# Two unused tiles ahead of the operands of a convolution's matrix products

## The chip, the core and the metric

The kernel runs on one core of a Trainium2 chip. The metric is the time of the whole program on the device in microseconds, from one launch, as the median of several runs. Before the change it is 2550.75 us (three runs, 2549.53 to 2551.24). A profile of one more execution comes with it. "PE" is the TensorE matrix engine, "PEld" the loading of its weights, "DVE", "ACT", "POOL" and "SP" are the vector, scalar, GpSimd and sync engines.

SBUF, the on-chip memory, has 128 partitions. A tile takes the same range of bytes in every partition, and "the start" of a tile is here always its byte in the partition.

## The reference

Three conv layers (and one small "interval" layer between the second and the third) act on x of 4 images, 32 x 32 pixels, 16 channels, each behind a group norm, each added back to x:

```python
first = jnp.einsum('ijyx,byxc->bijc', Msq, inputs)
kern = jnp.transpose(G, (0, 1, 5, 4, 2, 3)).reshape(h * w * f, c, G.shape[2], G.shape[3])
shifted = lax.conv_general_dilated(x_nchw, kern, STRIDES, PADDING)      # h*w*f = 16384 filters of 3x3x16
diff = jax.nn.relu(inputs[:, None, None, :, :, :] - shifted)
second = L * jnp.einsum('ijyx,bijyxc->bijc', Wsq, diff)
return first - second
```

So every one of the 1024 pixels (i, j) has 16 filters of its own (3 x 3 x 16 taps); each filter is run over the whole image, the difference to the image goes through a relu, and is summed over all pixels with a weight. The filters' products are nearly all the arithmetic.

## The kernel before

**Phases and steps.** There are 6 phases: 3 layers by 2 groups of two images. A phase has 8 chunks of 128 output pixels (t), a chunk 32 steps (f, b): one of 16 filters by one of the two images of the group. That is 6 x 8 x 32 = 1536 steps. A step computes the products of 128 filters (one for each pixel of the chunk, as the columns of the weights) with 1024 image positions, into a pair of PSUM banks `ps` (128 x 2 x 512).

**The products** (`products`, L591 to L606). The contraction over 9 x 16 = 144 taps and channels is held in 128 partitions, as two halves of 64 rows; half `h` of the rows makes one half of the image. Each product is one matmul with 64 rows, 128 weight columns and 512 moving columns (480 for one half of the last product), in the fp32r format. The two halves use different rows of the array and are issued one after the other. Numbers are split into a coarse and a fine part to keep precision, so a step has seven pairs of matmuls: `first_part` (L608) issues four pairs, weights WU and WL against the moving tiles `iy` and `iz`; then ACT scales the PSUM result (L628); one step later `second_part` (L631) issues three more, weights WD against `iyz` and W9 against `im9`, and DVE reduces the result with the relu and the weights `WT` in one instruction (L644). The order on PE is thus four pairs of step n, three pairs of step n-1, and so on, without a break. The first 16 steps use another form, with plain fp32 products from the tiles `first` and `raw` (L616).

**The moving operands** are the tiles `iy`, `iz`, `iyz` (for each of two groups 2 slots x 2 images x 512 floats, 8192 bytes) and `im9` (2 images x 512 floats, 4096 bytes), all from the pool `const`. They are computed once a phase from the tile `raw` (L120).

**The weights** of four filters are a unit. A unit has a tile `parts` (L217: 2 slots x 3 kinds x 4 filters x 128 floats, 12,288 bytes) and a tile `W9` (L218: 4 filters x 128 floats), three buffers of each, in the pool `wpool`, which also holds the loaded filters (`raw_u`, L107, two buffers) and the chunks `WT` (L113). A filter's weights of one kind are 512 bytes. `prep_parts` (L211) makes them from the loaded filters with ACT, DVE and POOL and two DMAs (L238), ahead of their use, and issues the next load (L108).

**Where tiles stand.** The pools take SBUF in the order in which they are opened, and within `const` tiles follow each other in the order of their lines. The program's own constants and a descriptor area come first, up to byte 16,512; then X (two tiles of 1024 bytes), XQ (1024) and raw (13,056). So `iy0` starts at 32,640. From there on, tile after tile of `const` up to L740 and later, then the pools `wpool`, `work`, `ivp` and `big`. `WT`, `W9`, `raw_u` and `parts` start at 101,824 and at whole multiples of 2048 from it. The last byte used is 223,296.

The lines that the change stands among:

```python
L120    raw = const.tile([P, 3, GB, PITCH], F32, name="raw")
L121    iy = [const.tile([P, 2, GB, NH], F32R, name=f"iy{g}") for g in range(NG)]
L124    im9 = [const.tile([P, GB, NH], F32R, name=f"im9{g}") for g in range(NG)]
L217            parts = wpool.tile([P, 2, 3, FU, P], F32R, tag="parts", bufs=AHEAD + 1, name=f"parts_{u}")
```

Of the kernel before, what the change touches and what calls it, by code (L numbers as in the profile page):

```python
# [8 lines left out]
F32 = mybir.dt.float32  # L9
# [6 lines left out]
P = 128  # L16
# [26 lines left out]
def net_kernel(ctx: ExitStack, tc: tile.TileContext, x, xq, xi, convs, iv_w, iv_b, out):  # L43
# [29 lines left out]
    const = ctx.enter_context(tc.tile_pool(name="const", bufs=1))  # L73
# [44 lines left out]


    raw = const.tile([P, 3, GB, PITCH], F32, name="raw")  # L120
    iy = [const.tile([P, 2, GB, NH], F32R, name=f"iy{g}") for g in range(NG)]  # L121
    iz = [const.tile([P, 2, GB, NH], F32R, name=f"iz{g}") for g in range(NG)]
    iyz = [const.tile([P, 2, GB, NH], F32R, name=f"iyz{g}") for g in range(NG)]
    im9 = [const.tile([P, GB, NH], F32R, name=f"im9{g}") for g in range(NG)]  # L124


    F0 = 2
# [819 lines left out]
```

## Time and profile before

| what | us |
|---|---|
| median of three runs | 2550.75 |
| the profiled execution's own time | 2549.96 |
| its span, first to last instruction | 2548.2 |
| PE busy in it | 2533.8 |
| PEld busy | 2182.0 |
| DVE busy | 2079.2 |
| ACT busy | 1893.1 |
| POOL busy | 1103.8 |

The span is what the views of the trace divide up; 1.8 us lie around it. Busy times are unions of overlapping instructions: the pipelined matmuls overlap each other, so the mean duration of a matmul (about 390 ns) is not the time from one to the next. For that one reads start times.

### The profile page before, as it was taken

To read this page: it belongs to the slowest core of one execution; us is meant where nothing else is said; L and a number is where in the kernel's file an instruction comes from. 1 tells how busy PE (TensorE), PEld (TensorE's weight loads), DVE (VectorE), ACT (ScalarE), POOL (GpSimd) and SP (SyncE) were. 2 spreads that over 40 slices of the span, in tenths; PEclk is the share of its full clock that TensorE was granted. 3 is DMA by queue.
4 is the path that set the end of the run, shared out by engine and by line. 5 is a ranking of instruction groups with operands and counts; after the bars stand their busy time and mean duration, and the time that the engine had idled before them with its cause. 6 is when DMAs were issued, how large, how long until landed. Compare 5 with 4: busy or idle time off the path is not lost.

```text
span 2548.2 us, 56662 instructions
## 1 busy us (share of the span) xinstructions
PE 2533.8 (99%) x21906; PEld 2182.0 (86%) x21906; DVE 2079.2 (82%) x3621; ACT 1893.1 (74%) x2181; POOL 1103.8 (43%) x990
## 2 busy tenths in 40 slices
PE   8999999999999999999999999999999999999999
PEld 5999888888888888998888888888888888888887
DVE  8887777888777887777788888888888887777777
ACT  4777777777777777777777777777777777777776
POOL 3445333453333434333345555454646344333332
PEclk9999999999999999999999999999999999999999
DMA  5556345464444654444454444554444466354442
GB/s 171 182 148 171 112 133 141 114 168 136 131 136 130 196 161 120 136 130 130 133 141 133 132 116 135 144 154 130 122 134 135 130 164 199 110 142 133 133 133 53
DMA packets 81182, 353.80 MB, mean 139 GB/s; under 512 B 18448, under 2 KB 20368, under 8 KB 80144
## 3 DMA queue, kind: packets, MB, share of 16 engines
q1 hardware_dynamic: 79920, 349.57, 49.0%
q8 instruction: 172, 2.82, 0.5%
q14 instruction: 98, 0.80, 0.1%
q10 hardware_dynamic: 864, 0.58, 0.1%
q0 software_dynamic: 128, 0.02, 0.0%
HBM read 199.19 MB, written 0.98 MB: 79 GB/s over the span
## 4 chain that ended last, share of the span: by engine, by line
PE 99%; ACT 0%; DVE 0%; issue 0%; POOL 0%; DVEq 0%; ACTq 0%; POOLq 0%
PE pc L599 98%; PE pf L396 1%; ACT pc L628 0%; PE ps_l L519 0%; PE ps_r L532 0%; DVE junk L644 0%; ACT L562 0%; ACT L324 0%; DVE raw L815 0%; PE ps_y L583 0%; DVE kept L759 0%; DVE kept L755 0%; PE ps_v L769 0%; DVE raw L823 0%; DVE squares L792 0%
## 5 line engine op out<-in xcount | busy, mean ns | idle before, releaser
L644 DVE SCALAR_TENSOR_TENSOR junk<-pc,WT 128x1024 f32<-128x1024 f32 x1536 | 1880.1, 1224 | 444.1 <-PE pc L599 404.3
L628 ACT ACTIVATE pc<-pc 128x1024 f32<-128x1024 f32 x1520 | 1531.8, 1008 | 621.9 <-PE pc L599 597.2
L599 PE MATMUL pc<-iyz,parts 64*128 64x512 f32 x6080 | 990.7, 393 | 1.8 <-ACT pc L628 1.8
L599 PE MATMUL pc<-iz,parts 64*128 64x512 f32 x6080 | 989.8, 392 | 0.0
L599 PE MATMUL pc<-iy,parts 64*128 64x512 f32 x6080 | 977.4, 390 | 0.0
L599 PEld LDWEIGHTS pc<-iyz,parts 64*128 64x128 f32 x6080 | 622.6, 185 | 96.7 <-ACT pc L628 5.6
L599 PEld LDWEIGHTS pc<-iz,parts 64*128 64x128 f32 x6080 | 619.9, 185 | 92.3
L599 PEld LDWEIGHTS pc<-iy,parts 64*128 64x128 f32 x6080 | 615.3, 185 | 90.2 <-issue 4.4
L228 POOL TENSOR_TENSOR parts<-raw,upper_w 128x512 fp32r<-128x512 f32 x190 | 246.7, 1298 | 1022.1 <-PE pc L599 863.0
L599 PE MATMUL pc<-im,W 64*128 64x512 f32 (+1 forms) x3072 | 631.9, 390 | 0.0
L599 PEld LDWEIGHTS pc<-im,W 64*128 64x128 f32 x3072 | 315.3, 185 | 49.8 <-issue 3.2
L229 POOL TENSOR_TENSOR W<-W,raw 128x512 fp32r<-128x512 f32 x190 | 247.9, 1305 | 2.0 <-ACT W L170 1.9
L232 POOL TENSOR_TENSOR parts<-parts 128x512 fp32r<-128x512 f32 x190 | 246.6, 1298 | 2.8 <-ACT parts L227 2.5
L205 POOL TENSOR_TENSOR raw<-raw,ident 128x512 f32<-128x512 f32 x190 | 201.1, 1059 | 43.1 <-DMA raw<-in_g 35.2
L170 ACT ACTIVATE W<-raw,low_w 128x512 fp32r<-128x512 f32 x190 | 136.1, 716 | 1.1 <-DMA raw<-in_g 1.1
L644 DVE DVE_READ_ACCUMULATOR junk<-pc,WT 128x1 f32 x1536 | 127.6, 83 | 0.0
L227 ACT ACTIVATE parts<-upper_w 128x512 fp32r<-128x512 f32 x190 | 118.7, 625 | 3.4 <-DVE upper_w L194 3.4
L231 ACT CAST parts<-upper_w 128x512 fp32r<-128x512 f32 x190 | 116.8, 615 | 0.0
L659 POOL TENSOR_SCALAR acc<-acc 128x32 f32<-128x32 f32 x40 | 11.5, 288 | 168.3 <-DVE junk L644 163.8
L194 DVE TENSOR_SCALAR upper_w<-raw 128x512 int32<-128x512 int32 x190 | 82.2, 433 | 0.2
L551 POOL TENSOR_TENSOR tables<-ft_b,rt 128x1089 f32<-128x1089 f32 x16 | 37.7, 2355 | 0.3 <-DVE s_b L558 0.3
L551 POOL TENSOR_TENSOR tables<-ft_a,rt 128x1089 f32<-128x1089 f32 x16 | 37.7, 2354 | 0.0
(138 smaller groups left out, 395.0 us busy)
## 6 DMA issues: line engine op xcount, KB each, us to landing
raw<-in_g SPq DMA_DIRECT2D x190, 768.0 KB, 7.2
parts<-parts SPq DMA_DIRECT2D x380, 384.0 KB, 5.0
WT<-in_w SPq DMA_DIRECT2D x48, 512.0 KB, 4.6
MT<-in_mt SPq DMA_DIRECT2D x6, 2048.0 KB, 13.5
raw<-xs SPq DMA_DIRECT2D x120, 67.8 KB, 2.6
raw<-in_xi SPq DMA_DIRECT2D x3, 271.0 KB, 5.0
raw<-in_xi SPq DMA_DIRECT2D x1, 813.0 KB, 6.9
xs<-xt SPq DMA_DIRECT2D x20, 34.0 KB, 2.3
```

Source lines behind the costliest of these rows:

```text
L170: nc.scalar.activation(dst, src, AF.Copy, scale=mask[:, 1:2])
L194: nc.vector.tensor_scalar(t.bitcast(I32), src.bitcast(I32), HIGH, None, op0=ALU.bitwise_and)
L205: eng.tensor_tensor(raws[u][:, s, at:to], raws[u][:, s, at:to], pick[s][:, f0 + at : f0 + to].unsqueeze(2).to_broadcast([P, to - at, P]), ...
L227: nc.scalar.activation(WD, high, AF.Copy, scale=-EPS)
L228: nc.gpsimd.tensor_tensor(WL, w8, high, ALU.subtract)
L229: nc.gpsimd.tensor_tensor(W9, W9.bitcast(F32), src[:, 2], ALU.add)
L231: nc.scalar.copy(WU, high)
L232: nc.gpsimd.tensor_tensor(WD, WD.bitcast(F32), WL.bitcast(F32), ALU.add)
L551: nc.gpsimd.tensor_tensor(t, ft[:, i, :].unsqueeze(1).to_broadcast([P, T1, T1]), rt, ALU.add,)
L599: nc.tensor.matmul(ps[:, half, :n], lhsT=w[r], rhs=v[r] if n == NH else v[r][:, :n], start=first and k == 0, stop=k == len(pairs) - 1, ski ...
L628: nc.scalar.activation(ps, ps, AF.Copy, scale=1.0 + EPS)
L644: nc.vector.scalar_tensor_tensor(junk, ps.rearrange("p h n -> p (h n)"), 0.0, chunks[n], op0=ALU.min, op1=ALU.mult, accum_out=accs[phase][ ...
```

## The change

A tile of 32 floats (128 bytes in each partition) is put behind `raw`, and one of 112 floats (448 bytes) behind `im9`. Nothing writes or reads them. No instruction is added, removed or moved in its engine's order; every tile behind a new one starts later by the bytes of it.

```diff
     raw = const.tile([P, 3, GB, PITCH], F32, name="raw")
+    const.tile([P, 32], F32, name="pad")
     iy = [const.tile([P, 2, GB, NH], F32R, name=f"iy{g}") for g in range(NG)]
     iz = [const.tile([P, 2, GB, NH], F32R, name=f"iz{g}") for g in range(NG)]
     iyz = [const.tile([P, 2, GB, NH], F32R, name=f"iyz{g}") for g in range(NG)]
     im9 = [const.tile([P, GB, NH], F32R, name=f"im9{g}") for g in range(NG)]
+    const.tile([P, 112], F32, name="pad_parts")
```

| tile | start before | over a multiple of 2048 / 512 | start after | over a multiple of 2048 / 512 |
|---|---|---|---|---|
| raw | 19,584 | 1152 / 128 | 19,584 | 1152 / 128 |
| iy0 (iy1, iz, iyz, im9 follow at multiples of 4096) | 32,640 | 1920 / 384 | 32,768 | 0 / 0 |
| WT (W9, raw_u, parts follow at multiples of 2048) | 101,824 | 1472 / 448 | 102,400 | 0 / 0 |
| acc, junk, upper | 165,344 and on | 1504 / 480 | 165,920 and on | 32 / 32 |
| first, MT (the pool `big`) | 190,528 | 64 / 64 | 191,104 | 640 / 128 |

The last byte used becomes 223,872.

## The prediction

> **What bounds the kernel now.** First the page: busy times (part 1) and the chain that ended last (part 4).
>
> ```profile
> PE 2533.8 (99%) x21906; PEld 2182.0 (86%) x21906; DVE 2079.2 (82%) x3621; ACT 1893.1 (74%) x2181; POOL 1103.8 (43%) x990
> ...
> PE 99%; ACT 0%; DVE 0%; issue 0%; POOL 0%; DVEq 0%; ACTq 0%; POOLq 0%
> ```
>
> PE is on the chain for 99% of the span: the time is the number of products times the distance from one to the next. Next the groups of PE by shape, for how many there are, and the longest waits of PEld, for who could hold PE up:
>
> ```profile
> L599 PE MATMUL pc<-iyz,parts 64*128 64x512 f32 x6080 | 990.7, 393 | 1.8 <-ACT pc L628 1.8
> L599 PE MATMUL pc<-iz,parts 64*128 64x512 f32 x6080 | 989.8, 392 | 0.0
> L599 PE MATMUL pc<-iy,parts 64*128 64x512 f32 x6080 | 977.4, 390 | 0.0
> ...
> L599 PE MATMUL pc<-im,W 64*128 64x512 f32 x1536 | 613.4, 399 | 0.0
> L599 PE MATMUL pc<-im,W 64*128 64x480 f32 x1536 | 585.2, 381 | 0.0
> ```
>
> ```profile
> PEld pc L599 <- issue: 18.6, 74, 0.7
> PEld pc L599 <- ACT pc L628: 5.6, 10, 0.8
> ...
> PEld pc L599 <- DMA parts<-parts: 0.4, 1, 0.4
> ```
>
> 3 x 6080 + 2 x 1536 = 21,312 products, so 10,656 pairs of row halves. Another engine or a DMA holds them up for some 10 us in all. The distance is read from a timeline of PE in a quiet stretch (start, duration, group; groups merged):
>
> ```profile
> 632.24 0.63 PE L599 MATMUL pc<-iy,parts 64*128 64x512 f32 x4
> 632.70 0.64 PE L599 MATMUL pc<-iz,parts 64*128 64x512 f32 x4
> 633.16 0.64 PE L599 MATMUL pc<-iyz,parts 64*128 64x512 f32 x4
> 633.63 0.40 PE L599 MATMUL pc<-im,W 64*128 64x512 f32 x2
> 633.86 0.63 PE L599 MATMUL pc<-iy,parts 64*128 64x512 f32 x4
> ...
> 635.48 0.63 PE L599 MATMUL pc<-iy,parts 64*128 64x512 f32 x4
> ```
>
> Steps begin at 632.24, 633.86 and 635.48: 1.62 us for seven pairs, 231.4 ns a pair. From the start times of all products I worked out the distance between the first `iy` products of a step and of the step after next: it is 3240 ns, to the nanosecond, in 1368 of 1530 cases. 10,656 x 231.4 = 2466 us of the span of 2548.2; the start, the interval layer's and the first terms' products and the tail are the rest.
>
> Last the windows, where other traffic varies (PE, PEld, DVE, ACT, POOL, clock, DMA share, GB/s):
>
> ```profile
> 300.00:400.00 100.00, 100.00 (x868) 84.76 (x866) 78.88 (x131) 75.56 (x87) 39.55 (x36) 1.00 0.46 129
> 500.00:600.00 100.00, 100.00 (x866) 84.47 (x864) 81.93 (x137) 77.92 (x91) 51.14 (x45) 1.00 0.56 151
> 800.00:900.00 100.00, 100.00 (x867) 84.72 (x865) 81.55 (x150) 74.56 (x86) 37.38 (x38) 1.00 0.60 180
> 1200.00:1300.00 100.00, 100.00 (x868) 89.99 (x866) 80.81 (x145) 75.35 (x86) 41.38 (x43) 1.00 0.47 133
> ```
>
> 866 to 868 products begin in each 100 us, with DMA at 0.46 or 0.60 and POOL at 37 or 51 us. The last row has another overlap of the weight loads of the two halves (90 us of PEld in place of 85), and the same rate.
>
> **What the Trainium skill says.** "SBUF — State Buffer", section "Who interferes with whom", says that PE never waits on another engine for SBUF; the windows agree. The same page, "Specifications (TRN2)", gives lines of 16 bytes as the unit of SBUF reads. The old starts, 1920 and 1472 over a multiple of 2048, are already multiples of 64, so by it nothing is gained; no run here tests coarser units. "TensorE: Matmul & The Clock Gate", section "LDWEIGHTS (loading the stationary operand)", gives columns / 1.2 ns for a weight load, 107 ns for 128; the trace has 185, start to end. Its section "Back-to-back issue gap" gives N / 2.4 + 2.5, 216 ns for 512 columns; the trace has 231.4. So 15 ns a pair, 164 us in all, are above what that page would have. If the change moves the time, it is out of these.
>
> **The change part by part.** *The tiles.* No instruction, DMA or wait is added, and none is moved in an engine's order: 0 us. The starts do become what is said: 32,640 + 128 is 16 x 2048, and 101,824 + 576 is 50 x 2048, with tiles that are themselves multiples of 2048. `WT`, `W9` and `raw_u` move along with `parts`.
>
> *DVE, ACT, POOL.* Their instructions on moved tiles (1224, 1008 and 1298 ns) might change by some ns. DVE has 18% of the span free, ACT 26%, POOL 57%, and PE hardly waits for them: 0 us. Without that cover, a DVE instruction 10 ns longer would cost 1536 x 10 ns = 15 us; it would have to grow by some 250 ns to use up its free time.
>
> *DMAs.* A load of `raw_u` lands in 7.2 us, and a unit lasts 8 x 1.62 = 13 us. A transfer could become shorter or longer by a good part and PE would see 0.4 us of it: 0 us.
>
> *The moving operands.* The trace before has only starts of 1920 over a multiple of 2048 here, so this must be bounded. Within this, tiles of group 0 and 1 lie 8192 bytes apart, slots 4096, images 2048. Sorted by these, the mean distances (of those under 260 ns) from one product of a half to its next agree within 0.01 ns for the two groups, and the sum of both halves' for the two images of the first product within 0.05. Higher address bits do nothing, then. For misaligned reads there are the plain products of the first 16 steps, whose rows of 32 floats lie 136 bytes apart. PEld there:
>
> ```profile
> 17.90 0.23 PEld L599 LDWEIGHTS pc<-raw,first 64*128 64x128 f32 x2
> 18.33 0.23 PEld L599 LDWEIGHTS pc<-raw,first 64*128 64x128 f32 x2 [0.20 <-issue]
> 18.76 0.23 PEld L599 LDWEIGHTS pc<-raw,first 64*128 64x128 f32 x2 [0.20 <-issue]
> ```
>
> A pair is 0.43 us, and each product has two records. "FP8 and Floating Point Precision", "TensorE Precision Notes", says that true FP32 takes four passes, so a record holds two and a pass of 512 columns takes 215 ns, though its rows start anywhere. That is less than the 231 here. I take 0; from below, removing all of the 15 ns would give -164 us; from above, +2.5 ns a pair (below).
>
> *The weights.* The four filters of a unit start at 1472, 1984, 448 and 960 over a multiple of 2048. One of them crosses a multiple of 2048 inside, the others don't. The mean distances for the four are 231.46, 231.46, 231.46 and 231.47 ns. What isn't seen is a start at a multiple of 512: all have 448 over it; the loads from `first` (64 over it) mostly take 186 ns in place of 185. All loads of 128 columns in this trace start 64 or 32 over a multiple of 128. A load starts 2 to 3 ns after the product before it on its half, and the next product 228 to 233 ns after that load's start, so a shorter load may well show in the distance. I take 0, and for the ends a load of 183 ns, the lower value that recurs in the trace (-2 ns a pair, -21 us), and +2.5 ns a pair (+27 us).
>
> The sum is 0. On the profiled execution this is 2549.96 us, 0.8 below the median; on the median, 2550.7.
>
> **How small is measurable.** About 0.2% (5.1 us) is what a measurement here can tell from no change. It is 0.48 ns a pair. So PE's rhythm is either untouched, or what it moves by will be seen.
>
> **Rivals.** *A: the weight load gets shorter.* A start at a multiple of 512 saves a part of the read, 185 to 183 ns. For: loads stand in the chain from product to product, and there are 15 ns above the page's gap. Against: `first` at another remainder has the same load time, and two different overlaps of loads give the same 3240 ns. Time: 2550.7 - 21 = 2529; up to 16 ns would be 2380, which needs the whole gap.
>
> *B, slower: the two reads of a half begin at the same place.* A load starts 2 to 3 ns after a product. Before, weights and moving operand stood 448 and 384 over a multiple of 512, 64 bytes apart; after, both at 0. If PE's two reads of the same partitions disturb each other at equal places, the start of each pair is late. Distances of 231 and 236 ns alternate already in the trace, so a step of 5 ns exists in this machinery. Price: half of the 231 become 236, 2.5 ns a pair, +27 us, 2577; all of them, about 2600. It decides from 0.48 ns a pair on. Against: the four places of a filter change the distance between the two reads by 512 bytes each with no effect[...].
>
> *C: transfers into the moved tiles take another time.* Hidden under a unit's 13 us: 2550.7, the same as the forecast.
>
> *D: the tiles don't stand where said.* Excluded by the sums above.
>
> **How the numbers follow.** No change 0.50 (C in it), A 0.20, B 0.30. I give B more than A because any disturbance of a rhythm that repeats to the nanosecond can lock it into a longer one, while A needs the load to be what is shortened. Within 0.2% is the first case. The range takes the first case, A down to a little below its price, and B up to its price of 2.5 ns: 2528 to 2578, which leaves out some 2 in 10 (a longer gain, or a step of more than 2.5 ns). The likeliest case alone would be 2549 to 2552.5.
>
> **What would show it.** Right: in the profile after, steps 1.62 us apart, 866 to 868 products per 100 us, loads of 185 ns. A: loads of 183 ns or fewer, steps of 1.606 us or less. B: loads of the same time, steps of 1.637 us or more, and more distances of 236 ns. If DVE, ACT or DMA stand in the chain of waits after, what I called hidden was not. I am wrong if the rhythm depends on address bits between 64 and 1024, which this trace cannot show.

## The result and the profile after

The changed kernel takes 2525.39 us (median of 4 runs, 2524.39 to 2525.67), against 2550.35 for the kernel before (4 runs); the ratio is 0.9902, with a 95% interval of 0.9889 to 0.9914. It is faster by 25 us, 1%. The forecast was no change; the time lies 2.6 us below the stated range.

The page of the changed kernel, busy times and the chain that ended last (lines are two further down in this kernel, so L599 is L601 here):

```profile
PE 2509.2 (99%) x21906; PEld 2186.7 (87%) x21906; DVE 2080.3 (82%) x3621; ACT 1890.2 (75%) x2181; POOL 1103.6 (44%) x990
...
PE 99%; ACT 0%; DVE 0%; issue 0%; POOL 0%; DVEq 0%; ACTq 0%; POOLq 0%
```

PE is still the whole chain, with the same number of instructions. Its busy time fell by 24.6 us, the span by 24.3; DVE, ACT and POOL are where they were. The longest waits of PEld in the changed kernel:

```profile
PEld pc L601 <- issue: 19.3, 73, 0.7
PEld pc L601 <- ACT pc L630: 5.8, 10, 0.8
```

PE's loads wait for other engines about as long as before. Next the timeline of PE, in a stretch that answers to that of before:

```profile
630.35 0.63 PE L601 MATMUL pc<-iy,parts 64*128 64x512 f32 x4
...
631.93 0.66 PE L601 MATMUL pc<-iy,parts 64*128 64x512 f32 x4
...
633.55 0.63 PE L601 MATMUL pc<-iy,parts 64*128 64x512 f32 x4
```

The steps now take 1.58 and 1.62 us in turn. There are 1520 steps of this form, so 1518 distances from a step to the step after next (the prediction's 1530 is 12 too many). They are 3206 or 3207 ns in 1378 cases, where it was 3240 in 1368. Of a step's two halves one has a product of 480 columns, and which half it is changes from step to step, so two steps are the unit in which the rhythm repeats. The mean of those 1378 is 3206.7 ns: 33.3 ns less for two steps, and 760 such pairs of steps make 25.3 us, the whole of the gain. The windows of the changed kernel, by the columns of before:

```profile
300.00:400.00 100.00, 100.00 (x876) 86.93 (x876) 79.65 (x133) 76.22 (x87) 39.58 (x36) 1.00 0.47 130
500.00:600.00 100.00, 100.00 (x874) 86.61 (x872) 82.83 (x139) 78.78 (x92) 51.26 (x46) 1.00 0.57 156
800.00:900.00 100.00, 100.00 (x877) 86.97 (x876) 82.80 (x157) 76.53 (x88) 40.55 (x37) 1.00 0.58 172
1200.00:1300.00 100.00, 100.00 (x877) 86.99 (x875) 83.03 (x156) 75.82 (x87) 39.81 (x41) 1.00 0.49 137
```

874 to 877 products begin in 100 us, where it was 866 to 868, with the granted clock at 1.00 in both and whatever the DMA share. So the gain is there throughout the run. It is not the same for all seven pairs of a step: in the start times, averaged over the undisturbed steps, the time from the second `iz` pair to the first `iyz` pair fell from 233.3 to 225.5 ns, and that from the first `iy` pair to the second rose from 229.7 to 233.7. The weight loads:

```profile
L601 PEld LDWEIGHTS pc<-iz,parts 64*128 64x128 f32 x6080 | 624.3, 184 | 85.7
L601 PEld LDWEIGHTS pc<-iy,parts 64*128 64x128 f32 x6080 | 619.6, 184 | 78.2 <-issue 4.4 <-DVE junk L646 2.1
```

These take 184 ns in place of 185. On these views rival A (shorter loads at multiples of 512) looks right, with its price of 21 us for 25. The experiments show that it isn't.

### The profile page after: what moved, and what is told of

Read it like the earlier page. It is cut to its first block, busy times and chain, and to the rows that moved or that the text cites. A ratio compares the mean times of both kernels' runs of the same rounds, so it can differ in the third digit from the quotient of the medians.

```text
span 2523.9 us, 56662 instructions
## 1 busy us (share of the span) xinstructions
PE 2509.2 (99%) x21906; PEld 2186.7 (87%) x21906; DVE 2080.3 (82%) x3621; ACT 1890.2 (75%) x2181; POOL 1103.6 (44%) x990
## 4 chain that ended last, share of the span: by engine, by line
PE 99%; ACT 0%; DVE 0%; issue 0%; POOL 0%; DVEq 0%; ACTq 0%; POOLq 0%
PE pc L601 97%; PE pf L398 1%; ACT pc L630 0%; DVE junk L646 0%; PE ps_l L521 0%; PE ps_r L534 0%; ACT L326 0%; ACT L564 0%; DVE raw L817 0%; PE ps_y L585 0%; DVE kept L761 0%; DVE kept L757 0%; PE ps_v L771 0%; DVE raw L825 0%; DVE squares L794 0%
## 5 line engine op out<-in xcount | busy, mean ns | idle before, releaser
L601 PE MATMUL pc<-iy,parts 64*128 64x512 f32 x6080 | 988.7, 393 | 0.1
L601 PE MATMUL pc<-iyz,parts 64*128 64x512 f32 x6080 | 971.8, 389 | 1.9 <-ACT pc L630 1.9
L601 PE MATMUL pc<-iz,parts 64*128 64x512 f32 x6080 | 968.3, 387 | 0.0
L601 PEld LDWEIGHTS pc<-iz,parts 64*128 64x128 f32 x6080 | 624.3, 184 | 85.7
L601 PEld LDWEIGHTS pc<-iyz,parts 64*128 64x128 f32 x6080 | 611.9, 184 | 89.1 <-ACT pc L630 5.8
L601 PEld LDWEIGHTS pc<-iy,parts 64*128 64x128 f32 x6080 | 619.6, 184 | 78.2 <-issue 4.4
L601 PE MATMUL pc<-im,W 64*128 64x480 f32 (+1 forms) x3072 | 623.4, 384 | 0.0
L601 PEld LDWEIGHTS pc<-im,W 64*128 64x128 f32 x3072 | 311.4, 185 | 46.3 <-issue 3.4
```

Of the source, the lines that this page charges most:

```text
L601: nc.tensor.matmul(ps[:, half, :n], lhsT=w[r], rhs=v[r] if n == NH else v[r][:, :n], start=first and k == 0, stop=k == len(pairs) - 1, ski ...
```

## The experiments

All edits are to the kernel before, and only move tiles; the arithmetic is untouched. "Distance" is the start of the weights minus the start of the moving operands. It was 64 bytes modulo 512, and became 0. "Two steps" is the mean of the distances from a step to the step after next that recur in the profile of the run, read from the start times of PE; two values are given where stretches of the same run differ, and a bracket where it takes four steps for the rhythm to repeat. Ratios are against the kernel before, with their 95% intervals.

### Which of the two alignments

Four kernels tell three theories from each other: that the alignment of the weights counts (W), that of the moving operands (M), or the distance of the two (D). Their edits, `pad` standing behind `raw` and `pad_parts` behind `im9` as in the change:

```diff
 moving only:      +    const.tile([P, 32], F32, name="pad")
 weights only:     +    const.tile([P, 16], F32, name="pad_parts")
 moving at 512:    +    const.tile([P, 160], F32, name="pad")
                   +    const.tile([P, 112], F32, name="pad_parts")
 same remainder:   +    const.tile([P, 112], F32, name="pad_parts")
```

Moving only:

> Only the first unused tile (128 bytes): the moving operands start at multiples of 2048, the weights at 64 over a multiple of 512. Theory W (the weight loads got shorter at multiples of 512): none of the gain, 2550 us, two steps take 3240 ns, loads 185 ns. Theory M (the moving reads start or run better at multiples of 2048 or 512): the whole gain, 2525 us, two steps take 3207 ns. Theory D (what counts is the distance between the starts of the two reads, modulo 512: 64 bytes before, 0 after; here it stays 64): no gain, 2550 us.

Weights only:

> Moving operands as before (1920 over a multiple of 2048), weights moved by 64 bytes to multiples of 512 (512-aligned, not all 2048-aligned). Theory W: the whole gain, 2525 us, 3207 ns for two steps, loads 184 ns. Theory M: no gain, 2550 us, 3240 ns. Theory D: the distance modulo 512 is 128 in place of 64 or 0; another time than either, or that of before, but not the full gain.

Moving at 512:

> Moving operands and weights both at 512 over a multiple of 2048, so both at multiples of 512. Theory W and theory D: the whole gain, 2525 us, 3207 ns for two steps. Theory M with a unit of 2048 bytes: no gain from the moving side, 2550 us, 3240 ns; theory M with a unit of 512 or less: 2525 us.

Same remainder:

> Only the second unused tile (448 bytes): moving operands and weights both at 384 over a multiple of 512, neither aligned, their distance modulo 512 is 0. Theory D: the whole gain, 2525 us, 3207 ns for two steps. Theory W: weights at no multiple of 512, no gain, 2550 us. Theory M: no gain, 2550 us.

| kernel | moving, over a multiple of 512 | weights, over a multiple of 512 | distance | us | ratio | two steps, ns |
|---|---|---|---|---|---|---|
| moving only | 0 | 64 | 64 | 2549.98 | 0.9998 (0.999 to 1.0007) | 3240 |
| weights only | 384 | 0 | 128 | 2553.11 | 1.0012 (1.0006 to 1.0019) | 3240 or 3250 |
| moving at 512 (of 2048) | 0 | 0 | 0 | 2526.40 | 0.9906 (0.9891 to 0.9921) | 3206.7 |
| same remainder | 384 | 384 | 0 | 2525.45 | 0.9904 (0.9887 to 0.992) | 3206.7 |

Theory D alone fits all four. The kernel with neither operand on a multiple of 512 has the whole gain; the two kernels with one of them aligned have none. Tiles of other engines move along with the weights in these kernels, but in every kernel of this document PE's loads wait only 5.5 to 5.9 us for ACT and 0.8 to 3.3 us for DVE's reduction in the whole run. The windows of "moving only" (distance 64, as before) and then of "same remainder" (distance 0, as after):

```profile
300.00:400.00 100.00, 100.00 (x868) 84.75 (x866) 78.97 (x131) 75.56 (x87) 39.55 (x36) 1.00 0.46 129
1200.00:1300.00 100.00, 100.00 (x868) 89.97 (x866) 80.84 (x145) 75.35 (x86) 41.44 (x43) 1.00 0.46 132
```

```profile
300.00:400.00 100.00, 100.00 (x876) 87.01 (x874) 79.43 (x134) 76.43 (x87) 39.59 (x36) 1.00 0.47 132
1200.00:1300.00 100.00, 100.00 (x876) 87.02 (x874) 83.23 (x155) 75.95 (x88) 40.90 (x42) 1.00 0.47 135
```

The first repeats the kernel before even in PEld's 84.8 and 90.0 us, the second the changed kernel. And the weight loads of "weights only", the kernel slower than before:

```profile
L600 PEld LDWEIGHTS pc<-iz,parts 64*128 64x128 f32 x6080 | 628.9, 184 | 95.8
L600 PEld LDWEIGHTS pc<-iy,parts 64*128 64x128 f32 x6080 | 626.1, 184 | 94.1 <-issue 4.4 <-DVE junk L645 1.0 <-DMA parts<-parts 0.2
```

Loads of 184 ns go with 2553 us as well as with 2525. So theory W, rival A of the prediction, is out.

### Which distances are fast

Only `pad_parts` is set here, with n floats of 120, 24, 32, 40, 48, 80 or 96, so the moving operands stay at 384 over a multiple of 512 and the distance is 64 + 4 n, modulo 512:

```diff
+    const.tile([P, n], F32, name="pad_parts")
```

> The weights stand 256 bytes behind the moving operands, modulo 512. If the distance counts modulo 256 (or a part of it that 256 is a multiple of): the time of distance 0, 2525 us and 3207 ns for two steps. If it counts modulo 512: another value, from the points so far (0: 2525, 64: 2550, 128: 2553) about 2550 to 2555 us.

> Distance 448, that is the weights 64 bytes before the moving operands. If the cost depends on how near the two reads are, whichever is ahead: the time of distance 64, 2550 us. If it depends on the order (the moving read[...] catches the weight read up when that is ahead of it): not that of 64; 2525 us or less, since here the moving read starts ahead. If distance 0 is fast only because both reads then ask for the same place in the same order: 2550 us or more.

> Distance 32. If the unit is 64 bytes: as 0 or as 64, 2525 or 2550 us. If the cost rises evenly with the distance: halfway, 2537 us and about 3223 ns for two steps.

> Distance 224 modulo 256, between the two fast points 192 and 0. If these are one fast stretch with a floor: 2525 us and 3207 ns for two steps. If 32-byte steps matter as they did from 0 to 32: another value, perhaps up to 2557 us.

> Distance 160 modulo 256, between 128 (2553 us) and 192 (2525 us). If the slow stretch runs from 32 to below 192: 2550 to 2557 us. If the fast stretch is half of the 256 bytes, that is 160 to 256: 2525 us. Halfway, 2540 us, if the cost falls evenly.

> Distance 192 modulo 512, weights and moving operands at multiples of 64. If the distance counts modulo 256: as 448, 2525 us and 3207 ns for two steps. If it counts modulo 512, with 0, 256 and 448 fast by chance: any other value, by the neighbours 128 and 160 (2553 and 2560) slow, 2550 us or more.

> Distance 384 modulo 512. If the distance counts modulo 256: as 128, 2553 us, 3249 ns. Modulo 512 and theory overlap: the run with 128 and 384 in turn took 3213 ns, 36 less than 128 alone, so 384 alone would be about 3178 ns, 2503 us.

| distance (modulo 256) | us | two steps, ns |
|---|---|---|
| 0 (0), changed kernel | 2525.39 | 3206.7 |
| 256 (0) | 2525.71 | 3206.7 |
| 32 | 2557.38 | 3250 (3245 to 3255 in turn) |
| 64, kernel before | 2550.35 | 3240 |
| 128, "weights only" | 2553.11 | 3240 or 3250 |
| 384 (128) | 2553.94 | 3240 or 3250 |
| 160 | 2559.84 | 3253.3 |
| 192 | 2526.41 | 3206.7 |
| 448 (192) | 2525.48 | 3206.7 |
| 224 | 2554.41 | 3246.7 |

The three pairs of kernels whose distances differ by 256 agree to within 1 us, so the distance counts modulo 256; the guess of 2503 us for 384 was wrong. 0 and 192 are fast, all others that were tried are slow; of the multiples of 32 only 96 was not tried. It is neither nearness nor order, and no even rise: 32 and 224, on both sides of 0, are slower than 64. In the three slowest kernels, at 32, 160 and 224, the weights stand off a multiple of 64, which might cost time by itself. Here both operands stand 32 bytes over a multiple of 64, at distance 0:

```diff
+    const.tile([P, 40], F32, name="pad")
...
+    const.tile([P, 112], F32, name="pad_parts")
```

> Distance 0, but weights and moving operands both start 32 bytes over a multiple of 64. If the distance alone counts: 2525 us, 3207 ns. If weights or moving operands off a multiple of 64 cost time in themselves (all three runs with weights off it, at distances 32, 160 and 224, took 2554 to 2560 us): 2550 us or more.

2525.53 us, ratio 0.9903 (0.9888 to 0.9918), two steps 3206.7 ns. So it doesn't. As long as all tiles share one distance, none of the alignments tried counts, not even that to 64 bytes; the distance does.

### Which two reads

The distance is between the weights and the moving operand of one product ("own"), or between the weights loaded for the next product and the moving operand that is read meanwhile ("overlap"). By the start times of before and after, a load mostly starts 2 to 4 ns after the product before it on its half, so the two overlap in time. As long as all tiles share one distance, own and overlap distance are the same. Six kernels give some pairs another; `pad` is 32 in all of them. In the first two the slots of `iy`, `iz`, `iyz` and `parts` stand 128 bytes further apart, and the weights start at 0 or at 128 over a multiple of 256 (`pad_parts` 112 or 144). `wide_slots` only gives the tile its old shape:

```diff
+    iy = [wide_slots(const.tile([P, 2, GB * NH + 32], F32R, name=f"iy{g}")) for g in range(NG)]
...
+            parts = wpool.tile(
+                [P, 2, 3 * FU * P + 32], F32R, tag="parts", bufs=AHEAD + 1, name=f"parts_{u}"
+            )
...
```

> As the changed kernel, but the second slot of iy, iz, iyz and of parts starts 128 bytes later, so weights and moving operand of every product have distance 0 modulo 256, while the weights of the next product have distance 128 to the moving operand read meanwhile in 6 of 7 pairs. Theory own: 2525 us, 3207 ns for two steps. Theory overlap: as distance 128 everywhere, less a seventh: about 2550 us, 3244 ns.

> The same tiles, with all weights 128 bytes later: every product has weights and moving operand at distance 128 modulo 256, while the weights of the next product have distance 0 to the moving operand read meanwhile in 6 of 7 pairs. Theory own: 2553 us, 3249 ns for two steps. Theory overlap: 2525 to 2529 us, 3207 to 3213 ns.

In the other four kernels a tile behind `iyz` (`pad_im9`) moves `im9`, or one behind `raw_u` (`gap`) moves `parts` back to a multiple of 256, so that of the weights W9 alone is off it, or both. The sizes for "W9 and im9 at 128" are below, with `pad_parts` 112. "W9 and im9 at 64" has `pad_im9` 16, `gap` 112 and `pad_parts` 112; "im9 at 384" has `pad_im9` 96, `pad_parts` 16 and no `gap`; "W9 at 128" has `pad_parts` 144, `gap` 96 and no `pad_im9`:

```diff
+    const.tile([P, 32], F32, name="pad_im9")
...
+        wpool.tile([P, 96], F32, tag="gap", bufs=1, name="gap")
```

> As the changed kernel, but W9 and im9 both start at 64 over a multiple of 512, everything else at 0. Theory own (the distance of weights and moving operand of the same product counts): all distances stay 0, 2525 us, 3207 ns for two steps. Theory overlap (the weights of the next product are read while the moving operand of this one is read, and the distance of these two counts): two of seven pairs have other distances (W9 is loaded while iyz is read: 64; WU while im9 is read: 448), so the time changes, by about 2/7 of 25 us if 448 is like 64: 2532 us.

> As the changed kernel, but im9 alone starts at 384 over a multiple of 512 (128 over one of 256). Its own weights W9 then have distance 128 to it, and so have the weights WU that are read while im9 is. Theory overlap, one pair of seven at the price of 128: (3249 - 3207) / 7 = 6 ns more for two steps, 2530 us; or 3200 ns and 2521 us, if it was this pair that made the run with the own distance 128 faster than the changed kernel. Theory own: 6 ns more, 2530 us.

> As the changed kernel, but W9 alone starts 128 bytes over a multiple of 256. Own distance 128 in one pair of seven (W9 and im9), overlap distance 128 in one (W9 loaded while iyz is read). Moving im9 alone by 128 cost 26.7 ns for two steps. If the own distance of W9 and im9 was its cause: again about 3233 ns, 2545 us. If it was the load of WU during im9: that is 0 here, so what counts is the load of W9 during iyz, another value than 3233, between 3200 and 3230.

> As the changed kernel, but W9 and im9 both start 128 bytes over a multiple of 256. The own distance is 0 again in all pairs, the overlap distance 128 in two. Theory own: 3207 ns, 2525 us. Theory overlap: the two pairs cost what they cost in the two runs with one of the tiles moved, 3233 ns or more, 2545 us or more.

| kernel | pairs with own distance not 0 | pairs with overlap distance not 0 | us | ratio | two steps, ns |
|---|---|---|---|---|---|
| slots apart, weights at 0 | none | 6, at 128 | 2531.09 | 0.9923 (0.9907 to 0.994) | 3213.3 (some 3197 and 3230 in turn) |
| slots apart, weights at 128 | all, at 128 | 1, at 128 | 2521.70 | 0.9886 (0.9871 to 0.9901) | 3200 |
| W9 and im9 at 64 | none | 1 at 64, 1 at 192 | 2526.17 | 0.9903 (0.9886 to 0.9919) | 3206.7 |
| im9 at 384 | 1, at 128 | 1, at 128 | 2544.36 | 0.9978 (0.9968 to 0.9988) | 3233.3 |
| W9 at 128 | 1, at 128 | 1, at 128 | 2533.92 | 0.9935 (0.9921 to 0.995) | 3213.3 or 3220 |
| W9 and im9 at 128 | none | 2, at 128 | 2543.02 | 0.9971 (0.9959 to 0.9982) | 3230 (3214 to 3246 in turn) |

Distances in this table are modulo 256. The own distance alone doesn't decide: with all own distances at 128 the kernel is the fastest of all, and with all at 0 "W9 and im9 at 128" is 18 us slower than the changed kernel.

The overlap distance gets these two right in direction, but it alone doesn't decide either. "Slots apart, weights at 128" and "im9 at 384" have the same overlap distances in all seven pairs: 128 where WU is loaded while `im9` is read, 0 in the other six. They take 2521.70 and 2544.36 us. Nor does a price for each pair, added up, work. About 2550 us was forecast for six pairs at overlap distance 128, and 2531 were measured; the prices of "im9 at 384" (26.7 ns for two steps) and "W9 at 128" (7 to 13 ns) don't add up to that of "W9 and im9 at 128" (23.3 ns); and with W9 and `im9` at 64, two pairs off 0 cost nothing (2526.17 us).

So where the two operands stand to each other sets the time, but which reads must be compared, and how they act on the rhythm, stays open. That the reads of a weight load and of a running product disturb each other is a guess that no run shows directly.

The kernel "slots apart, weights at 128" beats the kernel before and the changed one: its runs (2519.73 to 2522.24) lie below all of the changed kernel's, though the two were not timed side by side. Its windows, and then those of "im9 at 384":

```profile
300.00:400.00 100.00, 100.00 (x878) 85.94 (x877) 79.55 (x135) 76.54 (x87) 39.59 (x36) 1.00 0.47 134
1200.00:1300.00 100.00, 100.00 (x878) 85.29 (x876) 83.36 (x156) 76.25 (x88) 42.32 (x43) 1.00 0.46 131
```

```profile
300.00:400.00 100.00, 100.00 (x870) 83.24 (x868) 78.93 (x133) 75.71 (x87) 39.57 (x36) 1.00 0.45 128
1200.00:1300.00 100.00, 100.00 (x870) 94.14 (x868) 81.06 (x145) 75.84 (x88) 42.34 (x43) 1.00 0.46 128
```

878 products begin in 100 us in the first, one or two more than after the change, and 870 in the second.

## Why the prediction was wrong

- *What bounds the kernel*: right. The whole gain is PE's distance from pair to pair: 33.3 ns for 14 pairs are 2.4 ns a pair, and at 10.7 us for each ns that is 25 us.
- *DVE, ACT, POOL and DMAs at 0*: right. Their busy times changed by 3 us or less, and PE's loads still wait for other engines for little more than 10 us in all.
- *The moving operands at 0, the weights at 0*: each was right for itself within 0.2%, moved as the change moves it modulo 512 (ratios 0.9998 and 1.0012). The step that failed was adding them: 0 + 0 was taken as the cost of moving both. What counts is how the two stand to each other, which neither part has by itself. Going from distance 64 to 0 was worth 2.4 ns a pair, and the sum had no term for it.
- *The evidence on address bits*: groups, slots, images and the four filters differ by multiples of 512, and their equal times were read as "higher address bits do nothing". The measured unit is 256 bytes, so all these places have one distance, and the trace of before could say nothing about another. The prediction named address bits between 64 and 1024 as what it could not see, and still gave "no change" half of the chance.
- *The plain products as evidence*: the 215 ns for a pass are an estimate that no run here tests. They bear on reads that start anywhere, not on how far two reads stand apart.
- *Rival A*: near in time (2529 against 2525) by luck, since its cause is wrong. The loads did become 1 ns shorter, but they do so in a slower kernel too.
- *Rival B*: the right quantity, the distance of the two starts modulo a small unit, with the wrong sign: 0 is fast and 64 slow. Its counter-argument, that the four filters change the distance without effect, says nothing for the same reason as above.
- *Lines of 16 bytes*: the prediction took from the Trainium skill ("SBUF — State Buffer", "Specifications (TRN2)") that moving starts which are multiples of 64 gains nothing. The runs show a coarser unit, 256 bytes, and the page's lines don't explain the measured times: a shift of the weights by 32 bytes (distance 0 to 32) moved the time from 2525 to 2557 us.
- *The gap above 216 ns*: the gain is 2.4 of these 15 ns, and 13 are left (3206.7 / 14 = 229.0 ns). The Trainium skill ("TensorE: Matmul & The Clock Gate", "Back-to-back issue gap") gives its formula for a single product and says that in a stream of loads and products both set the spacing. So the 15 ns were no measure of what could go.

## What to carry to other kernels

In a stream of products like this one, each with a weight load of its own, the time can depend on where the two operands stand to each other, here modulo 256 bytes and by up to 1.3%, while the alignment of either, in the kernels with one distance for all, is without effect. A test of such a layout moves one operand alone over one period in small steps, and reads the distance of the products' starts from the trace, where 0.1% shows. Equal times for places that differ by a round number are no evidence that addresses don't matter: they may differ by whole periods.

## What was not expected of the hardware

Where all tiles share one distance, kernels with other absolute addresses repeat the rhythm of the product stream to the nanosecond: 3240 ns for two steps in both kernels at distance 64, and 3206.7 in all five at 0 or 256. The fast distances found are 0 and 192 modulo 256, with 32 and 224 beside 0, which are 40 to 43 ns slower for two steps. All that was found, 3200 to 3253.3 ns, spans 1.7%. Seven of the values (3200, 3206.7, 3213.3, 3233.3, 3240, 3246.7, 3253.3) stand at multiples of 6.7 ns from 3200. The distance doesn't always fix the rhythm: at 128 a kernel changes between 3240 and 3250 from one stretch to another within a run.
